# Two graph layers with routed experts on one core: full expert slots of the first block's rows move behind the last graph products

## The chip, the cores and the metric

The kernel runs on 1 core of one Trainium2 chip. The metric is the device time of one execution in microseconds (us); lower is better. The kernel before takes 1156.66 us (median of three runs, 1156.47 to 1158.17).

The engines are named as the profile names them: PE (TensorE matmul; PEld is its weight load), DVE (VectorE), ACT (ScalarE), POOL (GpSimd), SP (SyncE, which issues most of the DMAs). A "q" behind a name (SPq) is the engine's own instruction queue.

## The reference, cut to what matters

`x` is 3327 x 256, `adj` 3327 x 3327 with ones in about 0.5% of its places and on the diagonal. Two layers follow one another. Each has a graph step over all rows and an expert step in which every row goes to two experts.

```python
# layer 0: mean over neighbours; 16 experts, hidden 512, top 2
a = (adj == 1); x = x + ((a @ ln(x)) / a.sum(1)) @ W.T + b
h = ln(x); p = softmax(h @ gate_w + gate_b); top2, renormalised
x = x + sum over the 2 experts e of  weight_e * (silu(h @ w1[e]) * (h @ w2[e])) @ w3[e]
# layer 1: attention whose weights depend on the neighbour j alone after the softmax; 6 experts, hidden 256, top 2
Wh = ln(x) @ W;  x = x + leaky_relu(softmax(where(adj == 0, -1e9, el[:, None] + er[None, :])) @ Wh)
h = ln(x); router of two layers; top2
x = x + sum over the 2 experts of  weight_e * (relu(relu(h@w1[e]+b1[e]) @ w2[e] + b2[e]) @ w3[e] + b3[e])
```

## The kernel before, in words

Rows come in 26 tiles of 128 (25 full ones and one of 127), tiles in 7 chunks of four (the last has two), chunks in blocks: `GRAPH` is [chunks 0 to 2], [3, 4], [5], [6], so block 0 has 12 tiles.

**The graph step** (`graph`, called once for each layer) computes, for one block of result columns after the other, the product of the mask and the normalised rows `y`. `y` is held as two float32r parts, so each of 26 source tiles gives four 512-wide matmuls (line 528) to a chunk of the block. The mask comes as int32 from `adj_t` on SP's queue (`load_mask`, line 429, three `adj` buffers) and is turned into float32r on DVE (line 434, three `big` buffers). One load takes `max(1, 4 // len(block))` source tiles: one in block 0, two in block 1, four in the last two.

When a block is accumulated, its chunks' "post" work is spread among the next block's products: `finish` multiplies by W (line 481), adds to `xs`, normalises, stores the rows to `hd` and `xd` in DRAM, transposes (498); `after0`/`after1` compute the router's logits; `dispatch` finds the two experts and each row's place in its expert's list from the running counts `seen`, with matmuls (277 to 281) and DVE instructions (241 to 294), and writes 12 bytes for each row and expert to the list in DRAM, one indirect DMA for each tile and choice on POOL (line 297). The last block's post work has no products to run beside.

**The expert step** works in slots: 128 list entries of one expert in layer 0 (67 slots, of which 61 are used with these inputs), 256 in layer 1 (31 slots). `slot_table` (307 to 335) turns the final counts into a table: for slot s the expert, the place in the list, and whether the expert's weights must be loaded, or are still in the buffer that slot s - 2 (layer 0) or s - 3 (layer 1) used. SP reads the table with register loads (345, 346, 356). A slot then is: `places` (the list entries, line 357, on SP), `rows_in` (gather from `hd` on POOL, line 365), `turned` (transpose on PE, 377), `load` (weights on SP, 350: three times 512 KB in layer 0, 898 KB in layer 1), the matmuls (`hidden0` 679 and `out0` 694; `layer1` 783 and `out1` 793), and the result: in layer 0 a scatter-add to `xd` on POOL (line 384), which waits for the scatter-add before it, in layer 1 a scatter to `zd` (392). Weights have two buffers in layer 0 and three in layer 1.

PSUM's eight banks are two pools of four: `ps_acc` and `ps_mm`. `graph` accumulates chunks 0 and 1 of a block in `ps_acc` and chunk 2 in `ps_mm`.

**Order.** The program is written in the order of the text. The framework plans each engine's queue ahead of the run: of the instructions whose inputs are ready in its plan, the one that is written first goes first, so later work can be placed in gaps of earlier work. Each engine then executes its queue strictly in that order. `issue_after` pins one instruction behind another on its queue.

Of the kernel before, what the change touches and what calls it, by code (L numbers as in the profile page):

```python
# [25 lines left out]
def kernel(  # L26
# [50 lines left out]
    FAR = 1 << 20  # L77

# [4 lines left out]
    ps_mm = ctx.enter_context(tc.tile_pool(name="ps_mm", bufs=4, space=PSUM))  # L83
    ps_acc = ctx.enter_context(tc.tile_pool(name="ps_acc", bufs=4, space=PSUM))
# [7 lines left out]
    views = [dram_disjoint_views(li[:, :], 2 * NT) for li in lists]  # L92
    xd = dram.tile([NP + P, D], F32, name="xd")
    zd = dram.tile([2 * NP, D], F32, name="zd")
    zviews = dram_disjoint_views(zd[:, :], 2 * SLOTS1)
    def row_bc(v, name):
        n = v.shape[0]
        t = const.tile([P, n], F32, name=name)
        nc.scalar.dma_start(t, bass.AP(tensor=v.tensor, offset=v.offset, ap=[[0, P], [1, n]]))
        return t  # L100

    def by_chunk(w, name):
        t = const.tile([P, w.shape[0] // P, w.shape[1]], F32, name=name)
        nc.scalar.dma_start(t, w.rearrange("(k p) m -> p k m", p=P))
        return t
# [45 lines left out]
    def operands():  # L151

        small["w0"] = by_chunk(gnn0_wt, "w0t"), row_bc(gnn0_wt[DL, :], "w0r")
        small["w1"] = by_chunk(gnn1_w, "w1t"), row_bc(gnn1_w[DL, :], "w1r")
# [8 lines left out]
        for li in lists:  # L163
            nc.scalar.dma_start(li.rearrange("(p c) w -> p c w", p=P), idle[li.shape[0] // P])
        if N < NP:
            nc.scalar.dma_start(xd[N:NP, :], zrow[: NP - N, :])
            nc.scalar.dma_start(zd[2 * N :, :], zrow[: 2 * (NP - N), :])
# [4 lines left out]
    for i, li in enumerate(lists):  # L172
        n = li.shape[0] // P
        idle[n] = const.tile([P, n, 3], I32, name=f"idle{i}")
        nc.gpsimd.memset(idle[n], 0)
        at = idle[n][:, :, 0]
        if i == 0:
            nc.gpsimd.iota(at, pattern=[[1, n]], base=0, channel_multiplier=n)
# [124 lines left out]
    def slot_table(E, seen, size, slot_p):  # L303


        ps = ps_acc.tile([P, 512], F32, name="acc")
        nc.tensor.matmul(ps[:, :E], ones_h, seen, start=True, stop=True)

        def small(name, w=E, dtype=F32):
            return work.tile([P, w], dtype, name=name, bufs=1)  # L310
# [3 lines left out]
        nc.vector.tensor_scalar(nt, ps[:, :E], float(size - 1), None, op0=OP.add)  # L314
        nc.vector.tensor_scalar(nt, nt, size.bit_length() - 1, None, op0=OP.arith_shift_right)
        nc.vector.tensor_copy(d, nt)
        nc.vector.tensor_tensor_scan(end, ones[:, :E], d, 0.0, op0=OP.mult, op1=OP.add)
# [6 lines left out]
        nc.vector.tensor_tensor(hot, le[:, :E], le[:, 1:], op=OP.subtract)  # L324
        nc.vector.tensor_tensor(d, end, d, op=OP.subtract)
        nc.vector.scalar_tensor_tensor(d, d, -float(size), start_e[:, 0, :E], op0=OP.mult, op1=OP.add)
# [9 lines left out]
        return out  # L336
# [11 lines left out]
    def load(tile_, source, which):  # L348
        e, new = which
        nc.sync.dma_start(tile_, source(bass.ds(e, 1)), cond=new, bounds_check="skip_entire_dma")  # L350
# [9 lines left out]
    def rows_in(who):  # L360

        n = who.shape[1]
        xg = io.tile([P, n, D], F32, name="xg", bufs=5)
        for h in range(n):
            nc.gpsimd.indirect_dma_start(  # L365
                out=xg[:, h, :], out_offset=None, in_=hd,
# [4 lines left out]
    def turned(xg):  # L371

        n = xg.shape[1]
        ps = ps_mm.tile([P, KD, n * P], F32, name="mm")
# [7 lines left out]
    def rows_added(who, y):  # L382

        nc.gpsimd.indirect_dma_start(  # L384
            out=xd[:, :], out_offset=bass.IndirectOffsetOnAxis(ap=who[:, 0, 0:1], axis=0),
# [22 lines left out]
    def stream(blk):  # L408

        n, t0 = len(blk), blk[0]  # L410
        return xd[t0 * P : (t0 + n) * P, :].rearrange("(t p) d -> p t d", p=P), xs[:, t0 : t0 + n, :]
# [5 lines left out]
    def load_mask(adjs, big, block, g, value, op):  # L417
# [5 lines left out]
        def tile_of(pool, dtype, name):  # L423
            return pool.tile([P, 4 * BT * P], dtype, name=name)[:, : len(g) * ce].rearrange("p (t i) -> p t i", i=ce)
# [14 lines left out]
    def extended(w, r, name):  # L439

        t = const.tile([P, KD, D + 1], F32, name=name)
# [5 lines left out]
    def store(blk):  # L447
        to, x_ = stream([t for t in blk if t < NF])
# [417 lines left out]
```

## Time and profile before

| | |
|---|---|
| median of three runs | 1156.66 us |
| the profiled execution, its own time | 1151.96 us |
| its span, first to last instruction | 1150.2 us |
| busy in the span: PE / PEld | 994.0 / 854.8 us |
| DVE / ACT / POOL | 456.0 / 273.7 / 425.4 us |
| mean granted PE clock | 0.94 |
| first graph's products end, first slot's matmul | about 226 us, 271.15 us |
| layer 0's slots on PE end | about 657 us |
| second graph's products end, first slot's matmul | about 879 us, 927.79 us |

In the rows of the profile, `out<-in` are the program's tile names, and what follows `<-` in brackets is what ended the idle time before an instruction.

### The profile page before, as it was taken

What the parts mean: (1) busy time and instruction counts of PE and PEld (TensorE: products, weight loads), DVE (VectorE), ACT (ScalarE), POOL (GpSimd) and SP (SyncE); (2) the same over time, 40 slices, a digit from 0 to 9 for tenths busy, and PEclk for the clock granted to TensorE, in tenths of its full rate; (3) what the DMA queues carried; (4) which work ended last, traced back from release to release, by engine and by line L of the source; (5) the groups of instructions that cost most, each with busy time, mean ns of one, the idle gap of its engine ahead of it and who ended that gap; (6) DMA issues with size and microseconds to landing.
All of it is one profiled execution on the core that took longest, in us unless ns stands there. A gap on an engine that the chain in (4) does not pass through costs nothing.

```text
span 1150.2 us, 18163 instructions
## 1 busy us (share of the span) xinstructions
PE 994.0 (86%) x5644; PEld 854.8 (74%) x5644; DVE 456.0 (40%) x1667; ACT 273.7 (24%) x580; POOL 425.4 (37%) x403
## 2 busy tenths in 40 slices
PE   4989999816999999999999859999998179999950
PEld 3768777705999999999999847887766068888840
DVE  6646665650222222221222168476646402222225
ACT  2400212101111111111111135032232134444410
POOL 3000143543434443434435321002415456776620
PEclk9999999957999999999999979999999589999985
DMA  9978785545787786787675268966841065535527
GB/s 315 332 251 299 246 266 148 146 139 153 193 229 200 197 259 182 198 246 192 174 193 122 35 182 271 338 241 189 212 136 49 11 223 184 193 102 175 179 86 288
DMA packets 121080, 223.47 MB, mean 194 GB/s; under 512 B 33533, under 2 KB 70910, under 8 KB 120984
## 3 DMA queue, kind: packets, MB, share of 16 engines
q1 hardware_dynamic: 77360, 168.37, 44.5%
q0 software_dynamic: 22144, 32.69, 13.7%
q10 hardware_dynamic: 21480, 21.25, 6.0%
q8 instruction: 45, 0.74, 0.3%
q14 instruction: 51, 0.42, 0.1%
HBM read 259.77 MB, written 37.23 MB: 258 GB/s over the span
## 4 chain that ended last, share of the span: by engine, by line
PE 66%; DMA 15%; DVE 12%; issue 3%; ACT 2%; POOL 1%; SPq 1%; ACTq 0%; DVEq 0%; POOLq 0%
PE mm L679 20%; PE acc L528 14%; PE mm L783 9%; PE acc L694 9%; PE acc L793 4%; DMA adj<-in_adj_t 4%; DMA xd<-y,who 3%; PE mm L481 2%; PE mm L377 2%; DVE big L434 2%; DMA z<-zd 2%; DMA w<-in_ffn_w 2%; DMA xs<-in_x 2%; PE mm L551 1%; PE mm L528 1%
## 5 line engine op out<-in xcount | busy, mean ns | idle before, releaser
L528 PE MATMUL acc<-big,y 128*128 128x512 f32 (+3 forms) x1248 | 300.4, 387 | 37.6 <-DVE big L434 18.0
L528 PEld LDWEIGHTS acc<-big,y 128*128 128x128 f32 (+1 forms) x1248 | 221.0, 191 | 92.2 <-ACT y L739 16.8
L679 PE MATMUL mm<-xT,w 128*128 128x128 f32 x2144 | 265.7, 283 | 4.4 <-DMA w<-in_ffn_w 4.4
L679 PEld LDWEIGHTS mm<-xT,w 128*128 128x128 f32 x2144 | 260.3, 198 | 5.1 <-issue 5.1
L297 POOL DMA_INDIRECT list<-where,t_idx x104 | 110.0, 1058 | 266.6 <-DVE t_at L283 82.9
L384 POOL DMA_INDIRECT xd<-y,who x67 | 105.3, 1571 | 201.3 <-DMA xd<-y,who 101.6
L365 POOL DMA_INDIRECT xg<-hd,who x129 | 126.0, 976 | 74.6 <-issue 33.5
L687 DVE TENSOR_TENSOR hid<-hid,mm 128x512 f32<-128x512 f32 x67 | 46.1, 687 | 257.1 <-PE mm L679 257.1
L434 DVE TENSOR_SCALAR big<-adj 128x1536 fp32r<-128x1536 int32 (+5 forms) x112 | 107.8, 965 | 99.6 <-PE acc L528 58.5
L694 PE MATMUL acc<-w,hid 128*128 128x256 f32 x536 | 126.7, 380 | 0.0
L694 PEld LDWEIGHTS acc<-w,hid 128*128 128x128 f32 x536 | 96.9, 191 | 10.4
L379 ACT COPY xT<-mm 128x256 f32<-128x256 f32 (+1 forms) x98 | 43.1, 440 | 254.2 <-PE mm L377 210.1
L796 DVE TENSOR_TENSOR y<-acc,v 128x512 f32<-128x512 f32 x31 | 21.4, 692 | 157.0 <-PE acc L793 157.0
L784 ACT ACTIVATE h<-mm,v 128x256 f32<-128x256 f32 x124 | 58.7, 474 | 102.4 <-PE mm L783 102.4
L392 POOL DMA_INDIRECT zd<-y,who x62 | 62.0, 999 | 35.0 <-DVE y L798 18.5
L377 PE MATMUL mm<-ident,xg 128*128 128x128 f32 x258 | 47.4, 286 | 31.5 <-DMA xg<-hd,who 31.5
L377 PEld LDWEIGHTS mm<-ident,xg 128*128 128x128 f32 x258 | 45.7, 199 | 37.7 <-DMA xg<-hd,who 19.8
L783 PE MATMUL mm<-xT,v 128*128 128x256 f32 x248 | 65.9, 389 | 2.2 <-DMA v<-w1d 1.5
L683 ACT ACTIVATE hid<-mm 128x512 f32<-128x512 f32 x67 | 40.0, 597 | 106.6 <-PE mm L679 106.6
L783 PE MATMUL mm<-h,v 128*128 128x256 f32 x248 | 64.2, 381 | 1.3 <-ACT h L784 1.1
L793 PE MATMUL acc<-v,h 128*128 128x256 f32 x248 | 59.1, 380 | 0.1
L696 DVE TENSOR_SCALAR y<-acc,who 128x256 f32<-128x256 f32 x67 | 32.4, 484 | 66.3 <-PE acc L694 63.5
(167 smaller groups left out, 899.1 us busy)
## 6 DMA issues: line engine op xcount, KB each, us to landing
w<-in_ffn_w SPq DMA_DIRECT2D x201, 512.0 KB
adj<-in_adj_t SPq DMA_DIRECT2D x50, 768.0 KB
adj<-in_adj_t SPq DMA_DIRECT2D x36, 1024.0 KB
v<-w1d SPq DMA_DIRECT2D x31, 898.0 KB
hd<-ln_h ACTq DMA_DIRECT2D x12, 512.0 KB
z<-zd SPq DMA_DIRECT2D x6, 1024.0 KB
adj<-in_adj_t SPq DMA_DIRECT2D x12, 510.0 KB
w1d<-in_ffn_w ACTq DMA_DIRECT2D x18, 256.0 KB
```

The costliest lines, as they stand in the source:

```text
L297: nc.gpsimd.indirect_dma_start(out=rows_of[2 * (t0 + j) + i], out_offset=bass.IndirectOffsetOnAxis(ap=idx[:, i, j : j + 1], axis=0), in_=w ...
L365: nc.gpsimd.indirect_dma_start(out=xg[:, h, :], out_offset=None, in_=hd, in_offset=bass.IndirectOffsetOnAxis(ap=who[:, h, 1:2], axis=0),)
L377: nc.tensor.transpose(ps[:, k, h * P : (h + 1) * P], xg[:, h, k:D:KD], ident)
L384: nc.gpsimd.indirect_dma_start(out=xd[:, :], out_offset=bass.IndirectOffsetOnAxis(ap=who[:, 0, 0:1], axis=0), in_=y, in_offset=None, compu ...
L392: nc.gpsimd.indirect_dma_start(out=zviews[n * s + h], out_offset=bass.IndirectOffsetOnAxis(ap=who[:, h, 0:1], axis=0), in_=y[:, h, :], in_ ...
L434: nc.vector.tensor_scalar(mask[:kr, :, :cols], a[:kr, :, :cols], value, None, op0=op)
L528: nc.tensor.matmul(acc[c][k][:, :w], y[:kr, j, part, k * P : (k + 1) * P], mask[:kr, jj, i0 : i0 + w], start=(j == 0 and part == 0), stop= ...
L679: nc.tensor.matmul(q[:, c, :], w[:, k, h0 : h0 + 2 * P - 1 : 2], xT[:, k, :], start=(k == 0), stop=(k == KD - 1))
L694: nc.tensor.matmul(ps[:, :D], hid[:, c, :], w3[:, c // 2, c % 2, :], start=(c == 0), stop=(c == NC0 - 1))
L783: nc.tensor.matmul(ps[:, c, :], w[:, k, c : H1 : NC1], src[:, k, :], start=(k == 0), stop=(k == 1))
L784: nc.scalar.activation(dst[:, c, :], ps[:, c, :], AF.Relu, bias=w1s[s % 3][:, BB + 2 * i + c : BB + 2 * i + c + 1])
L793: nc.tensor.matmul(ps[:, h, :], h2[:, c, h * P : (h + 1) * P], w[:, c, :], start=(c == 0), stop=(c == NC1 - 1))
```

## The change

The first NE = 12 tiles (block 0) are routed before block 2's products begin. At that point the new version makes a first slot table from the counts so far. It holds full slots only: EARLY0 = ceil((3072 - 16 x 127) / 128) = 9 in layer 0 and EARLY1 = ceil((3072 - 6 x 255) / 256) = 7 in layer 1, the least number of full slots that any routing gives. Their list entries are read there (`routed0`, `routed1`), and they gather from the part of `hd` that block 0 stored (`hd_of[0]`) and add to the same part of `xd`. A second table, made after the graph as before, subtracts what the first has taken (`taken`). The number of slots stays. The slots themselves are still written after the graph.

PSUM is divided anew: two banks of `ps_mm`, and two for each of three accumulators (`ps_c`); early slots use accumulators 1 and 2, which blocks 2 and 3 leave free. In SBUF the slots' buffers are opened ahead of the graph, mask groups hold at most 1536 columns (one source tile in blocks 0 and 1, three in block 2, six in block 3), some buffer counts are smaller, the graph weights are staged in `w0[1]`, and the lists are cleared from a tile of 26 entries to a partition.

```diff
+    MASK = len(GRAPH[0]) * BT * P
+    NE = sum(map(len, GRAPH[0]))
+    EARLY0 = -(-(2 * NE * P - E0 * (P - 1)) // P)
+    EARLY1 = -(-(2 * NE * P - E1 * (S1 - 1)) // S1)
...
-    ps_mm = ctx.enter_context(tc.tile_pool(name="ps_mm", bufs=4, space=PSUM))
-    ps_acc = ctx.enter_context(tc.tile_pool(name="ps_acc", bufs=4, space=PSUM))
+    ps_mm = ctx.enter_context(tc.tile_pool(name="ps_mm", bufs=2, space=PSUM))
+    ps_c = [ctx.enter_context(tc.tile_pool(name=f"ps_{c}", bufs=2, space=PSUM)) for c in range(3)]
...
+    hd_of = dram_disjoint_views(hd[:, :], 2)
+    xd_of = dram_disjoint_views(xd[:, :], 2)
...
-            nc.scalar.dma_start(li.rearrange("(p c) w -> p c w", p=P), idle[li.shape[0] // P])
+            n = li.shape[0] // NP
+            nc.scalar.dma_start(li[: n * NP, :].rearrange("(b p c) w -> p b (c w)", b=n, p=P),
+                                idle[n].rearrange("p c w -> p (c w)")[:, None, :].to_broadcast([P, n, 3 * NT]))
...
-        idle[n] = const.tile([P, n, 3], I32, name=f"idle{i}")
+        idle[n] = const.tile([P, NT, 3], I32, name=f"idle{i}")
...
-    def slot_table(E, seen, size, slot_p):
+    def slot_table(E, seen, size, slot_p, first=None, taken=None):
...
-        nc.vector.tensor_scalar(nt, ps[:, :E], float(size - 1), None, op0=OP.add)
+        nc.vector.tensor_scalar(nt, ps[:, :E], float(0 if first else size - 1), None, op0=OP.add)
...
+        if taken is not None:
+            nc.vector.tensor_tensor(d, d, taken, op=OP.subtract)
...
+        if first:
+            had = small("s_had")
+            nc.vector.tensor_scalar(had, d, -1.0, float(first), op0=OP.mult, op1=OP.add)
+            nc.vector.tensor_scalar(had, had, 0.0, None, op0=OP.max)
+            nc.vector.tensor_tensor(had, had, own, op=OP.min)
+        if taken is not None:
+            nc.vector.tensor_tensor(d, d, taken, op=OP.subtract)
...
     def load(tile_, source, which):
         e, new = which
-        nc.sync.dma_start(tile_, source(bass.ds(e, 1)), cond=new, bounds_check="skip_entire_dma")
+        last["who"] = nc.sync.dma_start(tile_, source(bass.ds(e, 1)), cond=new, bounds_check="skip_entire_dma")
...
+    def bank(c, shape):
+        return ps_c[c].tile(shape, F32, name=f"acc{c}") if c >= 0 else ps_mm.tile(shape, F32, name="mm")
...
-            tmp = st.enter_context(tc.tile_pool(name=f"tmp{name}", bufs=2))
+            tmp = st.enter_context(tc.tile_pool(name=f"tmp{name}", bufs=4))
...
             for b, block in enumerate(GRAPH):
-                group = max(1, 4 // len(block))
+                group = MASK // (-(-min(sum(map(len, block)) * P, N - block[0][0] * P) // 2) * 2)
...
+                if b == 2:
+                    routed()
                 acc = {}
                 for c, blk in enumerate(block):
-                    pool, nm = (ps_acc, "acc") if c < 2 else (ps_mm, "mm")
-                    acc[c] = [pool.tile([P, BT * P], F32, name=nm) for _ in range(KD)]
+                    acc[c] = [ps_c[c].tile([P, BT * P], F32, name=f"acc{c}") for _ in range(KD)]
...
+    def routed0():
+        early["table"], early["had"] = slot_table(E0, seen0, P, slot_p, first=EARLY0)
+        for s in range(EARLY0):
+            who[s] = places(early["table"], s, E0, lists[0], P)
...
-            q = ps_mm.tile([P, NC0, P], F32, name="mm")
+            q = bank(2 if s < EARLY0 or s % 2 else 1, [P, NC0, P])
...
-        hid = io.tile([P, NC0, P], F32, name="hid")
+        hid = io.tile([P, NC0, P], F32, name="hid", bufs=2)
         silu = nc.scalar.activation(hid, ps[0], AF.Silu)
-        if s >= 8 and packs:
+        if s >= EARLY0 + 4 and packs:
...
-        ps = ps_acc.tile([P, 512], F32, name="acc")
+        ps = bank(1 if s < EARLY0 else 0, [P, 512])
...
-        rows_added(who, y)
+        rows_added(who, y, xd_of[0] if s < EARLY0 else xd)
...
+    graph("0", prepare0, 1.0, OP.is_equal, Later(0), update0, after0, 7, routed0, (operands_early, derived))
+    table0 = slot_table(E0, seen0, P, slot_p, taken=early["had"])
+    def table0_of(s):
+        return (early["table"], s) if s < EARLY0 else (table0, s - EARLY0)
...
-    for s in range(-5, SLOTS0 + 1):
-        if s + 5 < SLOTS0:
-            who[s + 5] = places(table0, s + 5, E0, lists[0], P)
-        if 0 <= s + 4 < SLOTS0:
-            xg[s + 4] = rows_in(who[s + 4])
+    for s in range(-4, SLOTS0 + 1):
+        known = EARLY0 if s < EARLY0 - 1 else SLOTS0
+        for i in range(max(who, default=-1) + 1, min(s + 6, known)):
+            who[i] = places(*table0_of(i), E0, lists[0], P)
+        for i in range(max(xg, default=-1) + 1, min(s + 5, known)):
+            xg[i] = rows_in(who[i], hd_of[0][: NE * P, :] if i < EARLY0 else hd[:, :])
         if 0 <= s + 1 < SLOTS0:
-            which[s + 1] = expert(table0, s + 1, E0)
+            which[s + 1] = expert(*table0_of(s + 1), E0)
             load0_hidden(s + 1, which[s + 1])
...
-    io = ctx.enter_context(tc.tile_pool(name="io1", bufs=3))
+    io = stage.enter_context(tc.tile_pool(name="io1", bufs=2))
...
-        ps = ps_mm.tile([P, NC1, S1], F32, name="mm")
+        ps = bank(2 if s < EARLY1 or i == 0 else 1, [P, NC1, S1])
...
```

Layer 1's loop is changed in the same way, with `known = EARLY1 if s < EARLY1 - 2 else SLOTS1`, list entries read up to four slots ahead and gathers up to three.

## The prediction

> **What bounds the kernel now.** I read the page's forty slices first, to see where TensorE (PE) is not full.
>
> ```profile
> PE   4989999816999999999999859999998179999950
> ...
> PEclk9999999957999999999999979999999589999985
> ```
>
> Slices 9 and 31 are holes: PE one tenth busy at half the clock. Outside them and the three dips (start, middle, end) PE is full, so little but filling holes can pay. The table of stages prices each hole (columns: window, its length, busy us of PE, PEld, DVE, ACT and POOL with their counts, clock, DMA share, GB/s).
>
> ```profile
> 97.00:169.00 72.00, 72.00 (x329) 54.75 (x330) 46.09 (x182) 13.13 (x26) 18.07 (x16) 1.00 0.77 252
> ...
> 202.00:226.00 24.00, 20.11 (x146) 17.89 (x145) 16.38 (x97) 4.29 (x9) 14.95 (x15) 1.00 0.46 112
> 226.00:271.00 45.00, 9.91 (x39) 4.51 (x37) 18.27 (x111) 5.26 (x12) 18.05 (x19) 0.60 0.50 156
> ...
> 861.00:880.00 19.00, 18.14 (x138) 16.56 (x137) 17.30 (x115) 3.90 (x12) 9.00 (x9) 1.00 0.28 70
> 880.00:928.00 48.00, 14.15 (x52) 6.80 (x53) 15.42 (x114) 8.83 (x21) 24.74 (x27) 0.64 0.19 48
> ```
>
> Idle PE: 45.00-9.91 = 35.1 us after the first graph's last product, 48.00-14.15 = 33.9 us after the second's; 69 us in all. What PE waits for stands in the timeline of the first hole:
>
> ```profile
> 227.68 0.97 DVE L434 TENSOR_SCALAR big<-adj 128x1536 fp32r<-128x1536 int32 x1 [1.32 <-DMA adj<-in_adj_t]
> ...
> 239.83 0.24 PE L279 MATMUL mm<-t_took,ones_h 128*128 128x48 bf16 x3 [9.07 <-DVE t_took L271]
> ...
> 252.38 0.17 PE L307 MATMUL acc<-seen,ones_h 128*128 128x16 bf16 x1 [0.36 <-DVE seen L287]
> 265.50 0.68 PE L377 MATMUL mm<-ident,xg 128*128 128x128 f32 x2 [12.95 <-DMA xg<-hd,who]
> ```
>
> It is one latency chain: routing of the last chunks on DVE, the slot table (L307), list reads, gathers, weights. Nothing else may run, because a slot needs the counts of all rows. The chain of waits gives the first weights and the slot rhythm:
>
> ```profile
> 266.37 4.64 DMA w<-in_ffn_w
> 271.15 5.97 PE mm L679 x32
> 277.12 0.23 PE mm L377 x2
> 277.34 3.77 PE mm L679 x32
> 281.11 1.73 PE acc L694 x8
> 282.84 0.23 PE mm L377 x2
> 283.07 3.77 PE mm L679 x32
> ```
>
> A slot of layer 0 costs 283.07-277.34 = 5.73 us of PE; in layer 1 the same chain has x16 groups at 955.95 and 961.62, so 5.67.
>
> **What moves.** Nine of 67 slots of layer 0 (9 x 5.73 = 51.6 us) and seven of 31 of layer 1 (7 x 5.67 = 39.7) no longer need the last counts. Both exceed their hole, so the holes cap the gain: 35.1+33.9 = 69.0. The number of slots is as before. Can they be ready? Chunk 2's list writes end on POOL at 186.5 (row at 184.83 lasting 1.70), landing 2.2 us later; nine list reads at 0.97 (five took 4.87 from 260.02) end near 197.5, and weights take 4.64: about 203, 23 us ahead of the hole. In layer 1 POOL sat idle 28.0 us before 868.56, so those writes were over at 840.5. The early slots are written after the whole graph in the program, but order in a queue follows readiness: the row at 227.68 is a mask of the second graph, which the program writes after every slot, and it ran before the first slot. Some also fits into the ragged ends 202-226 (3.9 idle) and 861-880 (0.9); I take 2 of 4.8.
>
> **What it costs.**
> Weights: the first 12 tiles hold 3072 (row, expert) pairs; counted from the inputs each of 16 experts gets 140 to 235 of them, one full slot of 128, so each early slot loads its own expert, 3 x 512 KB = 1.57 MB, which the late slots load again: 14.2 MB. In 226-271 the DMA moved 156 GB/s (7.0 MB, 2.1 of it weights), in 202-226 112. At the best start slice's 332 there is room for (332x45-4900)+(220x24) = 15.3 MB, enough; at 252 (97-169) 9.8 MB, short 4.4 MB or 17 us. 0 to 17; I take 4, since the wanted 275 GB/s lies nearer the 332 that the start holds.
> The scatter-adds wait for one another on POOL:
>
> ```profile
> 557.74 1.58 POOL L384 DMA_INDIRECT xd<-y,who  x1 [3.89 <-DMA xd<-y,who]
> 564.25 1.57 POOL L384 DMA_INDIRECT xd<-y,who  x1 [3.64 <-DVE hid L687]
> 568.90 1.58 POOL L384 DMA_INDIRECT xd<-y,who  x1 [1.80 <-DMA xd<-y,who]
> 573.48 1.57 POOL L384 DMA_INDIRECT xd<-y,who  x1 [1.72 <-DMA xd<-y,who]
> ```
>
> Intervals are 6.5 with weights in flight, 4.6 without. Today two of four slots load: 22.2 per four against PE's 22.9. Afterwards eleven slots in a row load (11 x 0.8 = 8.8 us of lag), then two of three (17.6 against 17.2; 9 experts x 0.4 = 3.6). Of 12.4 us the three y buffers hide one to two slots, 5.7 to 11.5. 0 to 20 (at 8.3, the longest interval, 11 x 2.6 = 28 less 8); I take 4.
> Hand-over to slot 9: the late table, ready at 256, is wanted about 287 (226+9.9+51.6), but its five list reads (4.9), read landing (4.0) and gather (4.1) stand behind slot 8's loads on SP, which start two slots (11.5) ahead: 2 (0 to 10).
> Layer 1 on POOL: two gathers and two scatters a slot at about 1.28 are 5.1 us, seven slots 36; three slots' gathers can precede (7.6), two slots' scatters trail (5.2); with 19 list writes at 1.27 (24.1; rows from 880.75 to 912.66) that is 47 in a hole of 48. Late list writes queued behind a scatter that waits for PE delay the late table, whose cover is only 880+14.2+39.7-927.8 = 6 us. 5 (0 to 15). Expert loads there, 18 slots in a row: one such slot today took 950.89-944.31 = 6.6, 0.9 over; 3 (0 to 16).
> SP queue: the first table read and the nine list reads are put ahead of mask loads; a wait there holds the masks of blocks 2 and 3. Two layers: 3 (0 to 2 x 19, chunk 2's list landing at 188.7 less block 2's start, about 169).
> Mask groups and banks: block 1 goes from 1 MB to 512 KB loads. DVE: 12 more mask instructions a layer; from 1226 ns at 2048 and 956 at 1536 columns the fixed part is 0.15 us, 2 us beside a DVE that is busy 46 of 72, nothing on the path. The nearest rows for loads of that size are 202-226 (16% idle) and 861-880 (5%), for larger ones 97-169 (0%). Over two 72 us blocks 0 to 23; with two product banks in place of four, for which no row exists (-1 to 7, a bank's wait at most 0.5 us for 14 chunks), I take 4: the ends of those windows have other causes too, the switch between blocks above all.
> Start: the list fill goes out in pieces of 26 x 12 = 312 B in place of 418 x 12 = 5016; the chain holds it for 8.02 us (29.16). 2 (-2, as POOL clears 78 words in place of 1254, to 8). The Trainium skill, DMA: Bandwidth & Descriptors, section Specifications, speaks against this edit: below 512 B the engine does read-modify-write. As an estimate that doubles the fill and the start term would be 8, the total 6 us later; no run here shows it.
> The second slot table, some 26 DVE instructions of 0.17 to 0.2 (252.61 to 256.2 now), runs under block 2's products, DVE being busy 20 of 33 there: 0; uncovered 5 a layer.
>
> Sum: 69.0+2 - (4+4+2) - (5+3) - 3 - 4 - 2 = 44. The profiled execution took 1151.96 (span 1150.2, 1.8 around it), the median is 1156.66, 4.7 above: 1151.96-44 = 1108.0, so 1112.7 expected.
>
> **Rivals.** (a) Transfers pace the early slots: scatter-adds at 8.3 (9 x 2.6 = 23) and POOL at its 15. For: POOL is full by the count above. Against: the first slots today (283 to 318) keep 5.7 with four loaded. With the other terms (3+2+3+4+2 = 14) that is 71-23-15-14 = 19, so 1138. (b) Slower: a convoy on PE. Early matmuls stand between block 2's and 3's products while their weights wait on SP behind mask loads whose buffers these products free. An unprepared slot is exposed 4.8 (266.37 to 271.15) plus 5.97-3.77 = 2.2, 7.0 us; sixteen cost 112. Beside the other terms (POOL 5, hand-over 2, groups 4, start 2 = 13) it decides from (71-13)/16 = 3.6 us a slot; at 5 it is 71-13-80 = -22: 1179. For: SP waited 111.9 us in all for mask buffers. Against: PE waited for w only 3 times, 4.4 us, and 23 us of lead. (c) It doesn't do what it says: the early slots stay behind the last routing matmuls (252.4 and 907.6). Then 271.15-252.4 = 18.8 and 927.8-907.6 = 20.2, less 27: 12, so 1145. Against: the mask at 227.68.
>
> **Chances.** Forecast 0.64 (own range 1087 to 1130), (a) 0.20, (b) 0.10, (c) 0.06. All of (b) and 0.01 of (c)'s tail end slower; 0.02 fall within 0.2%, about what a measurement of this kernel can tell from no change (three runs spread 0.15%): faster 0.87, same 0.02, slower 0.11. The lower bound is the full 71 with no cost to speak of (1086); the upper takes in (a) and (c): 1085 to 1146.
>
> **What would show it.** Right: first L679 matmuls before 226, slices 9 and 31 at 8 or 9 with full clock, L679 in layer 0 ending near 620, no PE gap over 5 us at slot 9; late list writes within 6 us of where they stood after the last product. Wrong: PE waits ended by DMA w inside the products (b), by POOL or DMA xd in slots 0 to 20 (a), first L679 after the last L281 (c).

## The result, and the profile after

The changed kernel takes 1197.11 us (median of four runs, 1196.28 to 1198.84) beside 1157.41 us for the kernel before: the ratio is 1.0339, 95% interval 1.0314 to 1.0365, slower by 40 us where 44 us of gain were forecast. The profiled execution takes 1196.82 us, its span is 1195.0. The runs of the study fell on several chips: on some the kernel before takes 1157 to 1167 us, on others 1214 to 1217, so every run is read by its ratio to the kernel before, run beside it on the same chip.

The first view is the page's forty slices again, and they look as the forecast wanted them.

```profile
PE   5789989889788888889888994999988997999960
...
PEclk9899999999899999899999996999999998999985
```

Both holes, a 1 each in the row of before (the ninth slice and the thirty-second, which the prediction calls 31), are filled: apart from both ends and the 4 between the layers no slice is under 7, and the clock stays at 8 or 9 there. But the slices between the holes, nearly all nines before, are nearly all eights: that is layer 0's late slots. A fifth more time on a stage that nobody had meant to touch is what turned the sign.

The stages were read off the timelines of four kernels at the same landmarks (us; "pinned" and "banks alone, shared" are explained below, experiments 1 and 2). The last two columns come from another chip, where the kernel before takes 1166.56 us; the changed kernel's own profile there has a span of 1196.5 us, so a few us between a column on the left and one on the right can be the chip's.

| stage | before | changed | changed, pinned | before, banks alone, shared |
|---|---|---|---|---|
| start to the first post product | 100.3 | 108.0 | 109.0 | 101.5 |
| to block 1's first post product | 68.8 | 73.9 | 72.4 | 69.5 |
| to graph 0's last product | 56.8 | 63.0 | 64.5 | 56.7 |
| to the end of the tenth slot's out product | 108.5 | 83.8 | 81.8 | 110.4 |
| the other 57 slots of layer 0 | 323.3 | 389.0 | 332.5 | 328.4 |
| to graph 1's first product | 15.8 | 17.5 | 22.1 | 15.0 |
| to graph 1's last product | 205.8 | 215.0 | 215.4 | 211.0 |
| to layer 1's last out product | 230.3 | 204.3 | 204.6 | 239.3 |
| to the end | 40.6 | 40.5 | 40.6 | 40.9 |
| span | 1150.2 | 1195.0 | 1142.9 | 1172.7 |

Changed less before: the two stages with the holes give 24.7 and 26.0 us; the start, blocks 1 to 3 and graph 1 take 7.7, 5.1, 6.2, 1.7 and 9.2; the 57 late slots take 65.7. Together that is 44.8, the difference of the spans.

The table of stages, asked for the late slots alone, says what kind of loss this is (columns as in the prediction). First the kernel before, then the changed one, over the same 57 slots.

```profile
334.40:657.70 323.30, 322.60 (x2358) 310.53 (x2356) 66.08 (x113) 55.48 (x113) 138.89 (x108) 1.00 0.71 186
```

```profile
328.70:717.70 389.00, 340.53 (x2354) 321.53 (x2352) 66.93 (x115) 54.75 (x111) 137.89 (x107) 0.96 0.66 177
```

Before, PE sat idle for 0.7 us of 323. Now it is idle for 389.00-340.53 = 48.5 us, and the same matmuls (2358 and 2354 records) are busy for 18 us more, at a mean clock of 0.96 in place of 1.00. DMA share and GB/s went down, so PE is not waiting for bandwidth. The waits of the whole span name what for (the line of the transposes was 377 and is 409; total, times, longest):

```profile
PE mm L377 <- DMA xg<-hd,who: 31.5, 4, 14.6
```

```profile
POOL xd L416 <- DVE y L737: 207.5, 49, 8.5
...
PE mm L409 <- DMA xg<-hd,who: 60.6, 29, 6.6
...
POOL xd L416 <- DMA xd<-y,who: 33.8, 8, 7.6
```

Four waits for a gather have become 29, of which 25, 48.3 us in all, lie in the late slots. The two lines on POOL matter as much: a scatter-add now waits for the result `y` 49 times and for the landing of the scatter-add before it 8 times. Before, those were 12 times (41.6 us) and 36 times (101.6 us). So the scatter-adds, which were the tightest thing beside PE before, have become slack; and still the chain that ended last prints them at the top:

```profile
DMA xd<-y,who 22%; PE acc L564 9%; PE acc L837 9%; PE acc L847 4%; PE acc L720 3%; DMA adj<-in_adj_t 3%; DMA z<-zd 2%; DVE big L469 1%; PE acc L735 1%; PE mm L409 1%; PE mm L587 1%; DVE ln_st L221 1%; DMA xg<-hd,who 1%; DVE upd L798 1%; SPq L384 1%
```

Whoever read only that line would make the scatter-adds faster. One turn of the late slots in the changed kernel's timeline shows the loop that is behind both (PE, then DVE, POOL, and PE again):

```profile
562.04 1.89 PE L735 MATMUL acc<-w,hid 128*128 128x256 f32 x8
...
563.98 0.48 DVE L737 TENSOR_SCALAR y<-acc,who 128x256 f32<-128x256 f32 x1 [0.97 <-PE acc L735]
...
564.74 1.57 POOL L416 DMA_INDIRECT xd<-y,who  x1 [5.17 <-DVE y L737]
566.61 0.98 POOL L393 DMA_INDIRECT xg<-hd,who  x1 [0.30 <-issue]
...
569.50 0.27 PE L409 MATMUL mm<-ident,xg 128*128 128x128 f32 x1
573.46 0.45 PE L409 MATMUL mm<-ident,xg 128*128 128x128 f32 x1 [3.69 <-DMA xg<-hd,who]
573.71 5.41 PE L720 MATMUL acc<-xT,w 128*128 128x128 f32 x32
```

These are the out product, the result, the scatter-add of slot 42 (counted from zero), and behind it on POOL's queue the gather for slot 49. In both kernels the gather for slot s+7 stands behind the scatter-add of slot s. Then PE reaches the first transpose for slot 49, 5.8 us after slot 42's out product ended, and must wait 3.69 us. But slot 49's own matmuls start only at 601.72, 28 us later: PE waits for something that nobody needs yet, and everything behind it in its queue waits too. It is slot 45's matmuls that stand at 573.71, and they run at a lower clock, 5.41 us in place of the 3.93 of an undisturbed group. The clock is the last but two of the numbers in this window's row:

```profile
573.70:579.00 5.30, 5.30 (x34) 5.30 (x34) 0.00 (x0) 0.60 (x1) 0.00 (x0) 0.69 0.37 110
```

Counted from the timeline, the first of a slot's two transposes starts 28.0 us before the slot's hidden products on average (slots 20 to 65); in the kernel before it is 6.0.

That lead comes from the banks. Before, transposes and hidden products took turns in the four banks of `ps_mm`, two banks of hidden products to one of transposes, and the framework could never plan a transpose more than one slot ahead. In the changed kernel the late transposes have the two banks of `ps_mm` to themselves. In the planned queue of PE the two halves of a slot's transposes stand four and three groups of hidden products ahead of their own; before, and in the early slots, which share a pair of banks with the out products, it is one.

Of the signs that the prediction named: the first early matmul starts at 226.41 (named: before 226), the last late list write of layer 1 starts 43 us after the graph's last product in place of 33 (named: within 6 us of that), layer 0's slots end at 717.7 (named: 620), and at the hand-over PE waits 6.59 us (named: no more than 5):

```profile
309.89 0.70 PE L409 MATMUL mm<-ident,xg 128*128 128x128 f32 x2 [6.59 <-DMA xg<-hd,who]
```

### The profile page after: what moved, and what is told of

Same layout as the page of the kernel before. It is cut to its first block, busy times and chain, and to the rows that moved or that the text cites. A ratio compares the mean times of both kernels' runs of the same rounds, so it can differ in the third digit from the quotient of the medians.

```text
span 1195.0 us, 18130 instructions
## 1 busy us (share of the span) xinstructions
PE 1020.1 (85%) x5646; PEld 872.8 (73%) x5646; DVE 468.5 (39%) x1739; ACT 278.2 (23%) x584; POOL 424.0 (35%) x403
## 3 DMA queue, kind: packets, MB, share of 16 engines
q0 software_dynamic: 22144, 32.69, 12.7%
## 4 chain that ended last, share of the span: by engine, by line
PE 31%; DMA 30%; issue 12%; DVE 7%; SPq 1%; ACT 1%; POOL 1%; ACTq 1%; POOLq 0%; DVEq 0%
DMA xd<-y,who 22%; PE acc L564 9%; PE acc L837 9%; PE acc L847 4%; PE acc L720 3%; DMA adj<-in_adj_t 3%; DMA z<-zd 2%; DVE big L469 1%; PE acc L735 1%; PE mm L409 1%; PE mm L587 1%; DVE ln_st L221 1%; DMA xg<-hd,who 1%; DVE upd L798 1%; SPq L384 1%
## 5 line engine op out<-in xcount | busy, mean ns | idle before, releaser
L564 PE MATMUL acc<-big,y 128*128 128x512 f32 (+2 forms) x1456 | 349.1, 393 | 49.7 <-ACT y L617 19.2
L564 PEld LDWEIGHTS acc<-big,y 128*128 128x128 f32 (+1 forms) x1456 | 265.2, 194 | 111.6 <-ACT y L617 19.7
L720 PE MATMUL acc<-xT,w 128*128 128x128 f32 x2144 | 279.9, 291 | 0.0
L720 PEld LDWEIGHTS acc<-xT,w 128*128 128x128 f32 x2144 | 276.5, 207 | 1.4 <-issue 1.1
L728 DVE TENSOR_TENSOR hid<-hid,acc 128x512 f32<-128x512 f32 x67 | 46.0, 687 | 305.3 <-PE acc L720 305.2
L469 DVE TENSOR_SCALAR big<-adj 128x1536 fp32r<-128x1536 int32 (+8 forms) x136 | 112.7, 830 | 111.5 <-DMA adj<-in_adj_t 57.6
L735 PEld LDWEIGHTS acc<-w,hid 128*128 128x128 f32 x536 | 97.3, 191 | 10.4
L724 ACT ACTIVATE hid<-acc 128x512 f32<-128x512 f32 x67 | 40.0, 597 | 277.7 <-PE acc L720 276.2
L838 ACT ACTIVATE h<-acc,v 128x256 f32<-128x256 f32 x124 | 58.7, 473 | 101.1 <-PE acc L837 100.7
L837 PE MATMUL acc<-xT,v 128*128 128x256 f32 x248 | 66.4, 389 | 1.2 <-DMA v<-w1d 0.6
L837 PE MATMUL acc<-h,v 128*128 128x256 f32 x248 | 66.1, 388 | 0.6 <-ACT h L838 0.6
```

The costliest lines, as they stand in the source:

```text
L469: nc.vector.tensor_scalar(mask[:kr, :, :cols], a[:kr, :, :cols], value, None, op0=op)
L564: nc.tensor.matmul(acc[c][k][:, :w], y[:kr, j, part, k * P : (k + 1) * P], mask[:kr, jj, i0 : i0 + w], start=(j == 0 and part == 0), stop= ...
L720: nc.tensor.matmul(q[:, c, :], w[:, k, h0 : h0 + 2 * P - 1 : 2], xT[:, k, :], start=(k == 0), stop=(k == KD - 1))
L735: nc.tensor.matmul(ps[:, :D], hid[:, c, :], w3[:, c // 2, c % 2, :], start=(c == 0), stop=(c == NC0 - 1))
L837: nc.tensor.matmul(ps[:, c, :], w[:, k, c : H1 : NC1], src[:, k, :], start=(k == 0), stop=(k == 1))
L838: nc.scalar.activation(dst[:, c, :], ps[:, c, :], AF.Relu, bias=w1s[s % 3][:, BB + 2 * i + c : BB + 2 * i + c + 1])
```

## The experiments

Theory A: the late slots lose to the run-ahead of their transposes, which the division of the banks allows. Rival B: the scatter-adds set the pace, as the chain says. Rival C: the weights that are loaded twice do.

**1. The order pinned, the banks as changed.**

```diff
-            xT[s + 1] = turned(xg[s + 1], 1 if s + 1 < EARLY0 else -1)
+            with tc.issue_after(last["mm"].ins) if s + 1 >= EARLY0 else nullcontext():
+                xT[s + 1] = turned(xg[s + 1], 1 if s + 1 < EARLY0 else -1)
```

`last["mm"]` is the last hidden matmul written. 

> The changed kernel, with one order pinned: the PE transposes of a late layer-0 slot (L409 into the two ps_mm banks) may not be issued before the last hidden matmul of the slot before. Theory A (run-ahead: with two banks of their own the transposes of slots s+4 stand in PE's queue ahead of the matmuls of slot s, so PE waits there for gathers that themselves wait for scatter-adds, two slots per 14 us): the late slots go back from about 7 us to about 5.7, that is 58 slots x 1.1 to 1.25 = 64 to 72 us, and the time falls from 1197 to 1125 to 1135. Rival B (the chain of scatter-adds, one waiting for the landing of the one before, sets the 7 us; the order on PE is only a symptom): no change, 1195 to 1199. Rival C (the extra weight loads pace the slots): no change in the first twenty late slots, back to 5.7 only where no expert is loaded twice: 1170 to 1190.

Measured: 0.9938 (0.9894 to 0.9983), on a chip where the kernel before takes 1214 us: about 46 us less than the ratio 1.0339, where theory A said 64 to 72. Since that first ratio was from another chip, both kernels were run once more side by side, where the kernel before takes 1166.56 us.

> The changed kernel as it is, as the reference for the runs beside it on one chip: 1.030 to 1.037 of the kernel before, as measured first (1.0339).

> The changed kernel with the pin alone, on the chip of the changed kernel itself. If the run-ahead carries the late slots' whole slowness (57 slots at 6.8 in place of 5.85 us = 54 us, and the 6.6 us gap at the hand-over): 50 to 62 us less than the changed kernel beside it, ratio 0.982 to 0.990. If it carries less, as the ratio on the slower chip (0.9938) suggested: 0.990 to 0.998.

Measured: the changed kernel 1203.13 us, 1.0346 (1.0293 to 1.0400), the pinned one 1151.33 us, 0.9866 (0.9839 to 0.9893). One line of order is worth 51.8 us (50 to 62 expected) and turns a slower kernel into a faster one. Its late slots take 5.83 us, and its table of stages and waits read:

```profile
328.00:660.00 332.00, 324.90 (x2356) 312.11 (x2354) 66.74 (x114) 55.52 (x113) 138.08 (x107) 0.99 0.76 207
```

```profile
POOL xd L416 <- DMA xd<-y,who: 86.9, 30, 6.8
...
POOL xd L416 <- DVE y L737: 46.8, 13, 4.7
...
PE mm L409 <- DMA xg<-hd,who: 7.5, 2, 4.8
...
PE acc L720 <- DMA w<-in_ffn_w: 7.1, 7, 1.8
```

The scatter-adds wait for one another again, 30 times, and PE is 98% busy: B is refuted, the chain's 22% was a consequence. PE's waits for weights are 7.1 us in all: C is not it either. The 2 waits for a gather that are left are the slots' start and the hand-over, 4.82 us there.

**2. The banks alone, without early slots.** If A holds, the kernel before must fall ill from the division of the banks and nothing else.

```diff
-    ps_mm = ctx.enter_context(tc.tile_pool(name="ps_mm", bufs=4, space=PSUM))
-    ps_acc = ctx.enter_context(tc.tile_pool(name="ps_acc", bufs=4, space=PSUM))
+    ps_mm = ctx.enter_context(tc.tile_pool(name="ps_mm", bufs=2, space=PSUM))
+    ps_c = [ctx.enter_context(tc.tile_pool(name=f"ps_{c}", bufs=2, space=PSUM)) for c in range(3)]
...
-            q = ps_mm.tile([P, NC0, P], F32, name="mm")
+            q = bank(2 if s % 2 else 1, [P, NC0, P])
...
-        ps = ps_acc.tile([P, 512], F32, name="acc")
+        ps = bank(0, [P, 512])
```

> The kernel before, with the PSUM banks given out by use as the change does (two for the small products and the transposes, two for each of three uses; hidden on the second and third pair in turn, out on the first), and nothing else: no early slots, the same mask groups, fill and table. Theory A (run-ahead of the transposes): the slots of layer 0 slow from 5.73 to about 7, 67 x 1.2 = 80 us, and the time is 1220 to 1240. Rivals B and C (scatter-adds or doubled weight loads, both of which this kernel has as before): 1155 to 1162. The post steps of the graph blocks have half their banks too; from the prediction's bound, up to +7 in all of these cases.

Measured: 1.0807 (1.0740 to 1.0873), the largest loss of the study, 97 us where 63 to 83 were expected. Late slots take 6.88 us; the line for the transposes is the changed kernel's, only larger, since all 67 slots are late ones:

```profile
PE mm L380 <- DMA xg<-hd,who: 98.5, 43, 16.0
```

Then the same with the transposes of layer 0 in the out products' pair, `bank(0, ...)` in place of `ps_mm`, which takes the run-ahead away without a pin; run on both kinds of chip.

> The kernel before with the banks by use, the layer-0 transposes taking theirs from the pair of the out products, and nothing else of the change. It separates the two costs of the bank division. Theory A (the run-ahead is nearly all of it): slots at 5.7 to 5.9, and what is left is the halved number of banks in the graph stages; by the prediction's bound that is -1 to 7, ratio 0.999 to 1.006. If the graph stages pay more for two banks in place of four (the run with banks by use showed the post steps and the second graph some 30 us longer in all): 1.015 to 1.03. If the slots stay at 6.9, the run-ahead is not the cause: 1.07 to 1.08.

> The kernel before with banks by use and the layer-0 transposes on the out pair, once more, beside the others. If the graph stages' loss to two small-product banks belongs to the kernel: 1.012 to 1.020, and the second pair (1.0011) gave it back. If it belonged to the slower chip: 1.000 to 1.006.

Measured: 1.0169 (1.0128 to 1.0210) and 1.0091 (1.0060 to 1.0123). The slots are back at 5.73 and 5.76 us, with the transposes one group ahead. So the division of the banks cost two things: the slots' order, 6.4% (1.0807 to 1.0169, two chips on which the kernel before takes 1214 us), and 0.9 to 1.7% that is left when the order is mended. In the last column of the table most of that rest lies in graph 1 (5.2 us) and in the stage after it (9.0 us), and 5.1 us in the late slots.

**3. What the rest is: too few banks for the post steps, or for the accumulators?** Two edits of the last kernel. One gives the post steps' first product and their transposes the third accumulator's pair, which is idle after block 0 (`ps = bank(2, ...)` in `finish`). The other gives the last block's accumulators the second pair, so that they need not wait for the block before.

> The kernel before with the banks by use and the transposes of layer 0 on the out pair (ratio 1.0169), and the post steps of the graph blocks given a second pair: the first product and the transposes of the normed rows take the third block pair, which is idle after the first block; the routing keeps the two small-product banks. Theory D (two banks are too few for the post steps, so that their work runs into the products' masks and past the last product): most of the 1.7% comes back, ratio 1.000 to 1.006. Theory E (the accumulators are the cause: the last block must wait for the block before, since both take the first pair): no change, 1.013 to 1.021.

> The same kernel (ratio 1.0169) with the accumulators of the last graph block on the second pair in place of the first, so that they need not wait for the evacuation of the block before. Theory E: most of the 1.7% comes back, ratio 1.000 to 1.006. Theory D: at most the 1 to 3 us of one wait in each layer, 1.011 to 1.018.

Measured, both on one chip: 1.0011 (0.9983 to 1.0039) and 1.0091 (1.0055 to 1.0126), the latter also the ratio of the kernel without either edit, on another chip. The second pair for the post steps gives all of it back, the accumulators nothing: the four shared banks had been the post steps' buffers. In graph 1 the post product of the last block starts 7.9 us after the last product in the kernel before, 11.4 us with two banks, 5.2 us with the second pair.

**4. The mask groups alone**, on the kernel before.

> The kernel before, with the mask groups of the change alone (1536 columns a load in all blocks, so that block 1 loads 512 KB in place of 1 MB a mask). The changed kernel's block 1 took 5.1 us longer and blocks 2 and 3 took 6.5 longer. If the smaller loads are the cause of block 1's part: 4 to 10 slower (two layers), 1161 to 1167. If the banks or the early slots are: 1156 to 1159. It would be faster only if the smaller masks start the products sooner: down to 1154.

Measured: 0.9988 (0.9954 to 1.0021). The smaller loads cost nothing that this can see, on a chip where the kernel before takes 1214 us; on the others they were not run alone.

**5. The list fill.** Pieces of 52 entries in place of 26, and the 256 entries at the end of a list as four pieces of 52 and one of 48 in place of 128 pieces of two (24 bytes).

```diff
-            nc.scalar.dma_start(li[: n * NP, :].rearrange("(b p c) w -> p b (c w)", b=n, p=P),
-                                idle[n].rearrange("p c w -> p (c w)")[:, None, :].to_broadcast([P, n, 3 * NT]))
-            nc.scalar.dma_start(li[n * NP :, :].rearrange("(p c) w -> p c w", p=P), idle[n][:, :2, :])
+            nb = n // 2
+            nc.scalar.dma_start(li[: n * NP, :].rearrange("(b p c) w -> p b (c w)", b=nb, p=P),
+                                idle[n].rearrange("p c w -> p (c w)")[:, None, :].to_broadcast([P, nb, 6 * NT]))
+            nc.scalar.dma_start(li[n * NP : n * NP + 8 * NT, :].rearrange("(p c) w -> p c w", p=4), idle[n][:4])
+            nc.scalar.dma_start(li[n * NP + 8 * NT :, :].rearrange("(p c) w -> p c w", p=1), idle[n][4:5, : 2 * P - 8 * NT])
```

> The changed kernel, with the slot lists filled in pieces of 52 entries (624 bytes a partition) in place of 26 (312). The Trainium skill, DMA: Bandwidth & Descriptors, section Specifications, puts a read-modify-write below 512 bytes; by that rule the start gains most of the 7.7 us it lost: 1189 to 1192. If the fill's time goes by the number of pieces alone, half of the 13.3 us that ACT waits longer for the idle tile and the fill comes back: 1192 to 1194. If the start is late for another reason: 1196 to 1198.

> The changed kernel with the pin and the larger fill pieces, the reads as in the change. It splits the step from 0.9938 (pin) to 0.9822 (pin, fill, reads). If each does what its trace said, the fill gives 4 to 7 us and the reads the rest: 0.987 to 0.991. If the fill alone did it: 0.981 to 0.984. If the reads alone: 0.992 to 0.995.

Measured: 1.0320 (1.0256 to 1.0385) without the pin, which says nothing beside 1.0339 and 1.0346; with the pin 0.9817 (0.9784 to 0.9849) where the pin alone has 0.9866 on another chip, so about 0.5%, 6 us, though the intervals overlap. The profiles are clearer: the first post product comes at 103.9 in place of 109.0. ACT's rows show why; first the changed kernel, then the one with the pin and the larger pieces:

```profile
28.58 0.48 ACTq L175 DMA_DIRECT2D list<-idle  x1
29.61 6.42 ACTq L177 DMA_DIRECT2D list<-idle  x1
36.07 0.50 ACTq L175 DMA_DIRECT2D list<-idle  x1
36.61 2.30 ACTq L177 DMA_DIRECT2D list<-idle  x1
...
44.36 2.07 ACT L233 ACTIVATE ln_h<-xs,ln_nmr,ln_var 128x256 f32<-128x256 f32 x4 [24.90 <-DMA list<-idle]
```

```profile
28.75 0.54 ACTq L176 DMA_DIRECT2D list<-idle  x1
29.33 0.72 ACTq L178 DMA_DIRECT2D list<-idle  x1
...
40.17 2.07 ACT L236 ACTIVATE ln_h<-xs,ln_nmr,ln_var 128x256 f32<-128x256 f32 x4 [20.30 <-DMA hd<-zrow]
```

The DMAs in 24-byte pieces, issued behind the fill's first, held ACT's queue for 6.42 and 2.30 us, and ACT's next work started 4.2 us later than with the larger pieces. The Trainium skill, DMA: Bandwidth & Descriptors, section Specifications, says that the DMA engine does read-modify-write below 512 bytes; the prediction weighed that against this edit, and the loss is of the size of its estimate (7.7 us, estimate 8). The runs do not show that this rule is the cause: two sizes changed at once, and 312 and 24 bytes are both below it.

**6. The early list reads on SP.** In the changed kernel nine reads sit between mask loads and wait for the list writes of block 0 to land. First SP, then DVE, which needs the next mask, then PE:

```profile
165.43 18.02 SPq L464 DMA_DIRECT2D adj<-in_adj_t  x7
195.03 10.01 SPq L385 DMA_DIRECT2D who<-list  x9
205.15 1.40 SPq L464 DMA_DIRECT2D adj<-in_adj_t  x2
...
211.17 0.96 DVE L469 TENSOR_SCALAR big<-adj 128x1536 fp32r<-128x1536 int32 x1 [12.69 <-DMA adj<-in_adj_t]
...
212.19 2.08 PE L564 MATMUL acc<-big,y 128*128 128x512 f32 x4 [5.34 <-DVE big L469]
```

The edit pins the reads behind block 2's eighth and ninth load; `last["adj"]` is the last mask load written, and `reads` (`reads0`, `reads1`) holds the loop over `places` that stood in `routed`.

```diff
+    def reads0():
+        last["who"] = last["adj"]
+        for s in range(EARLY0):
+            who[s] = places(early["table"], s, E0, lists[0], P)
...
                     mask = load_mask(adjs, big, block, g, value, op)
+                    if b == 2 and g is groups[-2]:
+                        reads()
```

It ran with pin and fill, once for itself and once beside the kernel without it.

> The changed kernel with three edits: the late transposes pinned behind the last hidden matmul of the slot before (as in the run with the pin alone, ratio 0.9938 to the kernel before), the list fill in pieces of 624 bytes with no remainder in pieces of 24, and the nine (seven in layer 1) early list reads pinned on SP behind the eighth and ninth mask load of the third block instead of the seventh. If fill and reads are what delayed the graph stages: the fill gives back 4 us (its trace showed the first post matmul at 103.9 in place of 108.0), the reads 3 to 5 in each layer, together 10 to 14, ratio 0.982 to 0.986. If neither is on the path: 0.992 to 0.996.

> The changed kernel with pin, fill and the early list reads behind two more mask loads, beside the one without the last edit. If the reads hold masks that PE then waits for, 4 to 9 us faster than that one, ratio 0.974 to 0.979. If the early slots lose by the later reads what the masks gain: within 3 us of it, 0.980 to 0.984.

> The changed kernel with pin and fill alone, as the reference beside the run with the reads moved: 0.979 to 0.985, as before (0.9817).

Measured: 0.9822 (0.9775 to 0.9868), and side by side 0.9792 (0.9739 to 0.9845) with the reads moved, 0.9911 (0.9882 to 0.9941, outside what was expected of it) without: 1.2%, 12 us on the chip where the kernel before takes 1217 us. In the profile of the first of these PE's 5 us gap is gone: from 165 to 229 no wait of PE is over 1.5 us. In the profiles of the pair, from one chip, it takes 253.2-103.0 = 150.2 us from the first post product to graph 0's last product with the reads moved, and 261.3-103.1 = 158.2 without. About 2% below the kernel before is the best that the study reached. The kernel without the reads moved reached that as well, on another chip (0.9817, experiment 5), so it is the pair on one chip that shows what the reads are worth.

**7. Another cure, and one that was no cure.** The pin replaced by a shared bank, and the second pair for the post steps put into the changed kernel, with and without the reads moved.

> As the run with pin, fill and reads, but with the pin replaced by a bank: the late transposes of layer 0 take their bank from the pair that the out products use, so that one of them can't be planned ahead of the out product before it. If it is the run-ahead that costs, and not the particular cure, the late slots go at 5.7 to 5.9 us and the time is that of the pinned kernel, ratio 0.98 to 0.996. If sharing a bank with out0 adds a wait of its own (the transposes then wait for DVE to empty the out bank): 6.0 to 6.4 a slot, ratio 1.00 to 1.02.

> The changed kernel with pin, fill and reads moved (ratio 0.9822) and the post steps' second pair. If theory D holds and the early slots' hidden products, which take the same pair, do not get in the way: 8 to 18 us faster than without, ratio 0.967 to 0.976. If the early slots and the post steps block each other there: 0.982 to 1.00.

> The changed kernel with the pin, the larger fill pieces and the post steps' second pair, the reads as in the change. If the second pair is worth in it what it is worth without early slots: 0.966 to 0.974. If the early slots' hidden products, which share that pair, take it back: 0.979 to 0.985, as with pin and fill alone (0.9817) and as with the reads moved too (0.9815).

Measured: 0.9855 (0.9814 to 0.9895), so sharing does what the pin does, with late slots at 5.90 us beside 5.96. The second pair is no gain here: 0.9815 (0.9786 to 0.9845) with the reads moved, 0.9892 (0.9858 to 0.9926, outside both forecasts) without, beside 0.9817 without either. In the last but one of these the graph's products do end 3.9 us earlier (238.1 in place of 242.0), but the first early out product ends at 264.1 in place of 254.5, and in layer 1 at 933.5 in place of 908.5. Early hidden products take the same pair as the post steps, and what the post steps gain the early slots lose.

**8. What the early slots bring.** The pinned kernel with both early counts at zero.

> The changed kernel with the pin but without early slots: both early counts are zero, so there is no early table, no early reads, and all 67 and 31 slots run behind the counts of all rows, with the banks, mask groups and fill of the change. Its difference to the run with the pin alone (ratio 0.9938) is what the early slots bring by themselves. By the traces before and after, 35.5 us in layer 0 and 25.9 in layer 1, less 2 to 10 for list reads and doubled weights: 50 to 60 slower than the pinned kernel, ratio 1.036 to 1.045. If the early slots bring less because they disturb the graph products: 1.00 to 1.03.

Measured: 1.0220 (1.0173 to 1.0267) beside 0.9938 on another chip of the same speed: 2.8%, 34 us. That is not the 1.036 to 1.045 of slots that bring their full worth, but lies in the 1.00 to 1.03 of slots that disturb the graph products. On the chip where the kernel before takes 1166.56 us the pinned kernel and the one with banks alone, shared, differ by 0.9866 to 1.0091, 26 us, in spite of the slower start; by the table the start and block 1 are 10.4 us of the other sign, so 37 there.

## Why the prediction was wrong

The mechanism that it argued for is there: early slots run in the holes, none of the rivals named took place, and the slots bring 34 to 37 us where the prediction's terms for them (69.0 and 2, less 4, 4, 2, 5, 3 and 3) make 50. What failed is the step "mask groups and banks", 4 us: it counted no cost of the banks for the 57 slots that do not move. They took 65.7 us more, and 51.8 us of the whole time came back when the order of their transposes was pinned.

**That step looked for the wrong thing.** It asked how long a user would wait for a bank, in the graph's blocks alone ("a bank's wait at most 0.5 us for 14 chunks"), and said of the slots only that their number is as before. But a bank that is shared also fixes an order. In layer 0 the four common banks were what held the transposes one slot ahead of their products; with banks of their own they ran ahead to the point where each stood barely behind the gather that it needs. Experiments 1 and 2 price this from both sides: 51.8 us by mending it in the changed kernel, 6.4% by making it alone in the kernel before. The trace of before had what was needed to see it coming: the gather for slot s+7 behind the scatter-add of slot s, and that scatter-add itself late.

```profile
521.97 1.97 PE L694 MATMUL acc<-w,hid 128*128 128x256 f32 x8
...
534.56 1.58 POOL L384 DMA_INDIRECT xd<-y,who  x1 [3.77 <-DVE hid L687]
536.45 0.98 POOL L365 DMA_INDIRECT xg<-hd,who  x1 [0.30 <-issue]
...
547.28 0.39 PE L377 MATMUL mm<-ident,xg 128*128 128x128 f32 x2
```

The scatter-add of slot 42 starts at 534.56, 10.6 us after its out product's end at 523.94, and costs nothing, because the transposes for slot 49 come at 547.28, another 12.7 us later. The prediction counted slots as PE time and the scatter-adds' lag in y buffers, and never asked how many slots of lead the gathers had.

**The other half of the step, the graph stages,** was mis-sized: 4 us with bounds 0 to 23 and -1 to 7. The groups cost nothing that experiment 4 can see, the two banks 10.6 us (0.91% of 1166.56) and 20 us on the slower chip (experiments 2 and 3).

**Start:** 2 us, measured 7.7. The range's end, 8, was nearer. The row that the prediction used, 8.02 us for the fill in large pieces, did not show the second, smaller DMA that the edit adds.

**SP queue:** 3 us within 0 to 38, measured 12 us side by side (experiment 6), and 9 us between two chips (0.9892 to 0.9815, experiment 7). The mechanism was named, a wait that holds the masks of blocks 2 and 3; the list writes were put at 188.7, and the reads started at 195.03.

**Hand-over:** 2 us within 0 to 10, measured 6.59, and 4.82 with the pin, so most of it does not hang on the order.

**Weights and scatter-adds**, 4 + 4 within 0 to 17 and 0 to 20. No run separates the two. The pinned kernel's 57 late slots take 332.5-328.4 = 4.1 us more than those of the kernel with banks alone, shared, and the lag of the scatter-adds is paid behind them: the last one starts 11.1 us after the last out product (671.3 and 660.2) in place of 4.4 (670.9 and 666.5), and graph 1 starts 22.1-15.0 = 7.1 us later. That is 11 us against 8. Two readings behind these terms were loose: the 6.51 us between two scatter-adds ended with a wait for `hid` on DVE, not for a landing, and the wanted 275 GB/s leaves out the 112 GB/s that 202-226 already moved; with it, it is (4.9+2.7+14.2 MB)/69 us = 316. The layer 1 rhythm held: late slots there take 5.64 us in the pinned kernel (5.69 before).

**Layer 1 on POOL and its expert loads,** 5 + 3: the last late list write starts 43 us after the graph's last product in place of 33, so the prediction's sign, within 6 us, failed. What that cost by itself no run shows.

**Holes:** 35.1 and 33.9. In the changed kernel the stage with the second gives 26.0 against before, but in the pinned one 34.7 against the kernel with the same banks; the stage with the first 28.6 there. Of that, the early work takes back 7.8 us in graph 0's last blocks (64.5 against 56.7) and 4.4 in graph 1.

**The rivals.** (a) put the time at 1138; the pinned kernel's ratio makes 1141 of 1156.66, but not through transfers, whose waits on PE are 7.1 us in all. (b), the slower one, had PE convoyed by unprepared early slots; a convoy on PE it was, but of late slots, and by a lead that was too long rather than too short. The list of rivals had nothing on the 57 slots that the change does not move.

## What to carry to other kernels

Here a buffer pool that several steps shared was also a brake on how far each could run ahead in an in-order queue. Before splitting one, write down for each user what it waits for (here a gather behind another slot's scatter-add) and how far ahead of its use it stands, and if the split lets it run further, pin it. When a stage slows although nothing in it was edited, compare the distance between a producer and its consumer in the two timelines before believing the chain of waits: here it followed the loop round and printed the longest link (22%), not the link that closed it (1%).

## What the runs showed of the hardware

The Trainium skill, Perfetto Trace Analysis, section Optimizing Tensor Performance, has independent matmul groups rotate through different PSUM banks. The graph's post steps agree (two banks more give back 9 us), the slots do not: with banks of their own the transposes make a slot 6.88 us, in a shared pair 5.73. Here more room was no good to an instruction whose inputs came late.

A wait of a few us on PE also cost clock. Eight of the changed kernel's 57 late groups of 32 matmuls took 5.16 to 5.46 us in place of 3.93, and each stands behind a wait of 2.27 to 4.05 us (after the one of 3.69 the granted clock was 0.69). Behind the shorter waits, up to 2.23 us, no group was slower, nor behind one of 2.35. The eight make 11 of the 18 us by which PE was busier; the other 7 stand in the rows of the transposes.

The same kernel had a different ratio on the two kinds of chip: the pinned one 0.9866 and 0.9938. On the slower one layer 1's late slots take 6.1 to 6.8 us in place of 5.65, with and without early slots; what distinguishes these chips no run here shows.
